# Routing the last rows of a graph layer while the first expert already runs

## The chip, the cores and the metric

The kernel runs on one core of one Trainium2 chip, as one launch. The metric is the device time of an execution in microseconds (us); a time is given as the median of several executions. One execution was recorded by the hardware profiler; times inside it count from the start of its span. Engines: TensorE (PE; its weight loads are PEld), VectorE (DVE), ScalarE (ACT), GpSimd (POOL) and SyncE (SP), which issues transfers (DMA).

## The reference, cut to what matters

3125 nodes with 256 features each go through four stages, each added to its input:

```
x = x + gat(gat(gat(layernorm(x))))        # three attention layers over the edges, relu between
x = x + top2_experts(layernorm(x))         # 16 experts, hidden 512
x = x + relu(h @ W + sum_of_neighbours(h @ M))    with h = layernorm(x)
x = x + top1_expert(layernorm(x))          # 8 experts on a shared hidden layer of 1024
```

The second stage is the one that matters here:

```
logits = einsum('bsd,de->bse', x, gate_w) + gate_b
probs  = softmax(logits);  top_probs, top_idx = top_k(probs, 2), made to sum to 1
hidden = silu(x @ w1[e]) * (x @ w2[e]);    out = sum over the two experts of weight * hidden @ w3[e]
```

Everything is float32. With the inputs given, the 16 experts get between 306 and 473 of the 6250 (node, expert) pairs, expert 0 gets 473.

## The kernel before

**Attention.** The edges are held as a dense matrix of counts. The nodes that receive are cut into 13 groups (`GROUPS`): groups 0 to 11 of 256 nodes, and a small last one of 53. For a group the loop runs over 25 tiles of 128 sending nodes, the steps `s`. In a step VectorE makes `pm` (L1388), 128 senders by 256 receivers, the unnormalised attention, and TensorE multiplies it with the senders' features into `acc` (L1391), one product for each of the group's two tiles of 128 nodes; each product appears as two matmul records. The small group uses `few` instead (L1379, L1381, L1383), six senders' tiles at a time. Six buffers of `pm` let VectorE run ahead.

Work that follows a group is put into a list `later` with a step number, and is issued between the steps of the group after it: `divide` at step 8 (division by the sum of weights, in place of a softmax, and the addition of x, into `y_out`), and in the third layer `norm` at 9, `gate` at 11 and `send` at 14. The engines execute in the order in which this loop issues, each its own queue.

**Router.** `norm` takes mean and variance, and stores the group's x to `sums` in DRAM. `gate` makes the normalised `row`, transposes it, multiplies with the gate's weights (L638). `send` picks the two largest logits of 16, makes weights, counts in `pre` how many rows each expert has so far, gets each row's `rank` among its expert's rows by two matmuls (L661), turns it into a place `g_to` (L670), and writes each row to its places in `rows` in DRAM with indirect transfers of GpSimd (L677), two for each tile of 128 nodes. Every expert has its own stretch of places. ScalarE needs three functions with tables of their own here: Sqrt in `norm`, Exp in `send`, and SiLU in the experts.

**finish** sums the counts up, and works out by some twenty small VectorE operations (to L721) a table of extra places: expert e's first 384 rows (`EACH` = 3 tiles) are done with the expert itself, the others in slots of 64 between and behind the experts. While VectorE does this, 32 matmuls of `keep_warm` occupy TensorE (L558).

**Experts.** `routed_experts` goes through the experts 0 to 15. `turn(e)` loads 384 rows `xs` (L745, on SP) and transposes them (L750, L751). `first` multiplies with w1 and w2 in four pairs (j, u) of 128 hidden features (`ps_h`, L775, 32 records), and makes `hid` by SiLU (L778) and a product (L779). `second` multiplies with w3 (`ps_o`, L790), weights the result to `y` (L793), and adds its rows into `sums` by indirect transfers (L795), one for each tile. The weights of expert e are loaded by `fetch`, three transfers of 512 KB. When all are done, x is loaded back from `sums` for the third stage.

What is allocated from one pool waits for the last reader of the buffer that it takes over, transfers included. Groups of large blocks (`block(big)`, two of them) are shared by the stages in turn.

Of the kernel before, what the change touches and what calls it, by code (L numbers as in the profile page):

```python
# [22 lines left out]
P = 128  # L23
# [543 lines left out]
class Router:  # L567
# [6 lines left out]
    def __init__(self, tc, cp, ident, eps, iota, count, rows, sums, gate_w, gate_b, table):  # L574
        nc = self.nc = tc.nc
        self.table = table
        self.tc, self.ident, self.eps, self.iota, self.rows, self.sums = tc, ident, eps, iota, rows, sums
        self.before, self.every = count
        self.gw = cp.tile([P, KD, NX0], F32, name="gate_w")
        nc.sync.dma_start(self.gw, gate_w.rearrange("(k p) e -> p k e", p=P))  # L580
        self.gb = cp.tile([P, NX0], F32, name="gate_b")
        nc.sync.dma_start(self.gb, spread(gate_b, NX0))
        spare = cp.tile([P, D], F32, name="spare")
        nc.gpsimd.memset(spare, 0.0)
        for q in range(0, CAP0, P):
            nc.sync.dma_start(sums[NP + q:NP + q + P], spare)

        self.real = cp.tile([P, NT], F32, name="real")
        nc.gpsimd.memset(self.real, 1.0)
        nc.gpsimd.affine_select(self.real, self.real, pattern=[[-P, NT]], compare_op=OP.is_gt, fill=0.0, base=N,  # L590
                                channel_multiplier=-1)

        self.off = cp.tile([P, NT], F32, name="off")
        nc.vector.tensor_scalar(self.off, self.real, -float(NX0 * NP), float(NX0 * NP), op0=OP.mult, op1=OP.add)

        self.pre = cp.tile([P, NT + 1, NX0], BF16, name="pre0")
        nc.gpsimd.memset(self.pre[:, 0], 0.0)
        self.first = cp.tile([P, NX0], F32, name="first0")
        nc.gpsimd.iota(self.first, pattern=[[NP, NX0]], base=0, channel_multiplier=0,
                       allow_small_or_imprecise_dtypes=True)  # L600
        self.node = cp.tile([P, NT], F32, name="node0")
        nc.gpsimd.iota(self.node, pattern=[[P, NT]], base=0, channel_multiplier=1,
                       allow_small_or_imprecise_dtypes=True)

    def group(self, wp, rp, pp, x, t0, n):
# [7 lines left out]
        def norm():  # L613
            for i, t in enumerate(tiles):
                st = wp.tile([P, 6], F32, name="g_st")
                nc.vector.bn_stats(st, x[:, t])
                nc.vector.bn_aggr(mv[:, i], st)
            nc.scalar.activation(rstd[:, 1], mv[:, :, 1], AF.Sqrt, bias=self.eps)
            table(nc, wp, rstd[:, 1], AF.Exp)
            nc.vector.reciprocal(rstd[:, 0], rstd[:, 1])  # L620
            nc.sync.dma_start(self.sums[t0 * P:(t0 + n) * P].rearrange("(t p) f -> p t f", p=P), x[:, t0:t0 + n])
# [3 lines left out]
        def gate():  # L625
            pz = pp.tile([P, n, NX0], F32, name="ps_z")
            for i, t in enumerate(tiles):
                row = rp.tile([P, ROW0], F32, name="row")
                nc.vector.tensor_scalar(row[:, :D], x[:, t], mv[:, i, 0:1], rstd[:, 0, i:i + 1], op0=OP.subtract,
# [11 lines left out]
        def send():  # L641
# [7 lines left out]
            if t0 + n == NT - 1:  # L649
# [8 lines left out]
            for i, t in enumerate(tiles):  # L658
                nc.vector.tensor_tensor(self.pre[:, t + 1], self.pre[:, t], sel[:, i], op=OP.add)
            rank = pp.tile([P, n, NX0], F32, name="ps_z")  # L660
            nc.tensor.matmul(rank, self.before, sel, start=True, stop=False)  # L661
            nc.tensor.matmul(rank, self.every, self.pre[:, t0:t0 + n], start=False, stop=True)
# [18 lines left out]
        return norm, gate, send  # L681

    def finish(self, cp, pp, over):
# [5 lines left out]
        nc.scalar.copy(self.pre[0:1, 0], total)  # L689
        keep_warm(nc, pp.tile([P, (NT + 1) * NX0], F32, name="ps_x"), self.every, self.pre.rearrange("p t e -> p (t e)"), 32)  # L690
# [32 lines left out]

def routed_experts(tc, x, room, ident, rows, sums, places, w1, w2, w3, load):
# [10 lines left out]
    with tc.tile_pool(name="rw", bufs=3) as ep, tc.tile_pool(name="rx", bufs=2) as xp, \  # L735
# [5 lines left out]
        def turn(e):  # L741
            xs = xp.tile([P, nq, ROW0], F32, name="xs")
            for q, n in ((0, nq),) if e else ((0, 1), (1, 1), (2, nq - 2)):
# [10 lines left out]
        def fetch(e, behind):  # L754
# [3 lines left out]
            if 0 < e < 3:  # L758
# [3 lines left out]
            dma = (nc.sync if 0 < e < 3 else nc.scalar).dma_start  # L762
# [95 lines left out]
        turned = turn(0)  # L858
        behind = turned[1][:, 0, 0:1]
        for e in range(NX0):  # L860
            a, b, o = fetch(e, behind)
            if e == 2:
# [214 lines left out]
FINISH = [(0, 20), (2, 16), (4, 4), (5, 16)]  # L1077
TERMS = 18
# [96 lines left out]
def dense_attention(tc, dram, counts, x_in, big, ident, eps, layers, src, dst, rows, high, make_router, over, count):  # L1175
# [10 lines left out]
    with tc.tile_pool(name="dw", bufs=1) as cp, tc.tile_pool(name="dwl", bufs=2) as wl, \  # L1186
# [3 lines left out]
        with tc.tile_pool(name="dp", bufs=6) as pmp, tc.tile_pool(name="ds", bufs=2) as sp, \  # L1190
# [81 lines left out]
            def terms(now, a):  # L1272

                c, n = GROUPS[a]
# [36 lines left out]
            for i in range(3):  # L1311
                last = i == 2
                bt_i = bt
                if last:
# [4 lines left out]
                    y_out = block(big)  # L1319
                    nc.gpsimd.memset(y_out[:, NT - 1], 0.0)  # L1320
# [23 lines left out]
                for a, (c, n) in enumerate(GROUPS):  # L1344
                    if apart_now and a < APART:
                        continue
                    tiles = [(q, (c + q) // P, min(P, n - q)) for q in range(0, n, P)]

                    edges = counts_of(counts, a)
                    ahead = list(pairs[a + 1]) if i == 0 and a + 1 < len(GROUPS) else []  # L1350
                    ready = []
                    tau = tau_next or terms(now, a)
# [8 lines left out]
                    for s in range(NT):  # L1361
                        now_step[0] = (a - APART) * NT + s
                        if s == (EARLIER if apart_now else TERMS):
                            if a + 1 < len(GROUPS):
                                tau_next = terms(now, a + 1)
                            else:
                                tau_next = None if last else terms(nxt, 0 if apart_now else APART)
# [17 lines left out]
                        else:  # L1385
# [4 lines left out]
                            for j, (q, t, r) in enumerate(tiles):  # L1390
                                nc.tensor.matmul(acc[:r, j, :D + 1], pm[:, q:q + r], now.h[:, of, :D + 1], start=(s == 0),  # L1391
                                                 stop=(s == NT - 1))
                        while ready and ready[0][0] <= s:
# [22 lines left out]
                    def divide(tiles=tiles, acc=acc, rest=rest, b=bt_i, last=last):  # L1416
# [13 lines left out]
                        for j, (q, t, r) in enumerate(tiles):  # L1430
                            if last:
                                to, add = y_out[:r, t], rest[j][:r]
# [9 lines left out]
                    sooner = 2 if a == len(GROUPS) - 2 else 5 if i == 0 and a == len(GROUPS) - 1 else 0  # L1442
                    later.append((8 - sooner, divide))
                    if last:
                        norm, gate, send = router.group(wp, rp, zp, y_out, tiles[0][1], len(tiles))
                        later += [(9 - sooner, norm), (11 - sooner, gate), (14 - sooner, send)]
# [28 lines left out]
            for _, what in later:  # L1475
                what()
            router.finish(wp, zp, over)
# [8 lines left out]
    return y_out  # L1486
# [525 lines left out]
def routed(ctx: ExitStack, tc: tile.TileContext, i: dict, out: bass.AP, over):  # L2012
# [12 lines left out]
    with tc.tile_pool(name="counts", bufs=1) as kp:  # L2025
        counts = kp.tile([P, NT * ((len(GROUPS) - 1) * PAIR + 64)], U8, name="counts")
        x = dense_attention(tc, dram, counts, i["x"], big, ident, eps, layers, i["src"], i["dst"], (rows0, rows),
                            over[:, 3:4], lambda cp: Router(tc, cp, ident, eps, iota, count, rows0, sums,
                                                            i["L0_ffn_gate_w"], i["L0_ffn_gate_b"], more), over[:, 0:1], count)
        with tc.tile_pool(name="s0", bufs=1) as sp:  # L2030
            ws, wm = (sp.tile([P, KD, D], F32, name="s_" + n) for n in "WM")
            hidden = hidden_weights(nc, early, *(i["L1_ffn_" + n] for n in ("W1", "b1", "Wg", "bg")), x[:, 0, 0:1])
            room = block(big).rearrange("p t d -> p (t d)")
            xnT = room.rearrange("p (k n) -> p k n", k=KD)
            routed_experts(tc, x, room, ident, rows0, sums, more, *(i["L0_ffn_" + n] for n in ("w1", "w2", "w3")),
# [96 lines left out]
```

## Time and profile before

| | |
|---|---|
| median of 6 executions | 1898.14 us (1895.28 to 1901.55) |
| the profiled execution | 1903.16 us |
| its span | 1901.4 us |
| TensorE busy in the span | 1792.8 us, 94% |
| VectorE / ScalarE / GpSimd busy | 1018.2 / 725.8 / 489.7 us |
| mean granted TensorE clock | 0.976 |
| third layer's group 11, last matmul | ends 1073.2 us |
| small group's last matmul | ends 1080.4 us |
| first expert's first matmul | starts 1104.8 us |
| second expert's first matmul | starts 1122.9 us |

How to read the lines that follow. A line of a chain of waits is: start in us, duration, engine, what it writes, line of the program, number of instructions. A line of a table by stretches is: the stretch, its length, busy time and number of instructions of each engine, the clock that TensorE was granted (1.00 is full speed), the share of the DMA engines in use, GB/s. A line of a table of groups is: program line, engine, operation, tile written <- tiles read, shapes, number | busy us, mean ns of one | idle time of the engine just before, and what ended it. The busy time of matmul records overlaps with that of the next: from start to start they are shorter than their mean.

### The profile page before, as it was taken

How to read it: one execution, taken by the hardware profiler on the slowest of the kernel's cores; microseconds unless marked ns; L12 is line 12 of the kernel's file. 1: busy time of each engine (PE TensorE's matmuls, PEld its weight loads, DVE VectorE, ACT ScalarE, POOL GpSimd, SP SyncE). 2: the span in 40 equal slices, each digit the busy share in tenths (PEclk: the TensorE clock that was granted, in tenths of full speed). 3: DMA queues.
4: the chain of work that ended last, by engine and by line, in shares of the span. 5: the costliest groups of instructions: out<-in, count | busy, mean ns of one | idle time of the engine just before them, and what ended most of it. 6: DMA issues, size and time to landing. Idle time of an engine off the chain costs nothing. (4 is left out here: it accounts for less than half of the span.)

```text
span 1901.4 us, 27323 instructions
## 1 busy us (share of the span) xinstructions
PE 1792.8 (94%) x9249; PEld 1400.3 (74%) x9249; DVE 1018.2 (54%) x2865; ACT 725.8 (38%) x2078; POOL 489.7 (26%) x636
## 2 busy tenths in 40 slices
PE   6999999999698888999999799999989999999997
PEld 4788888887576777788888666666668887555886
DVE  6888888875376666677777622222244222324221
ACT  3767666761001011222222211121127999444221
POOL 4210110000665655023333322333310000132122
PEclk9999999999799989999999999999999999999999
DMA  3111214766332323121111175877430000743764
GB/s 114 32 46 49 82 45 172 300 247 237 82 89 76 88 69 81 32 57 45 45 46 45 68 233 151 248 194 193 106 87 1 1 1 1 240 159 125 226 210 126
DMA packets 118370, 211.50 MB, mean 111 GB/s; under 512 B 14843, under 2 KB 80929, under 8 KB 118184
## 3 DMA queue, kind: packets, MB, share of 16 engines
q1 hardware_dynamic: 78228, 130.30, 20.4%
q0 software_dynamic: 24848, 56.84, 11.5%
q10 hardware_dynamic: 15138, 22.44, 3.6%
q8 instruction: 79, 1.29, 0.3%
q14 instruction: 77, 0.63, 0.1%
HBM read 118.61 MB, written 93.00 MB: 111 GB/s over the span
## 5 line engine op out<-in xcount | busy, mean ns | idle before, releaser
L1391 PE MATMUL acc<-big,pm 128*128 128x257 f32 x3400 | 798.0, 386 | 17.0 <-issue 13.3
L1391 PEld LDWEIGHTS acc<-big,pm 128*128 128x128 f32 x3400 | 634.9, 192 | 111.4 <-issue 17.3
L1388 DVE SCALAR_TENSOR_TENSOR pm<-tau,big,counts 128x256 f32<-128x256 f32 x850 | 397.3, 485 | 144.5 <-PE acc L1391 111.6
L1933 POOL DMA_INDIRECT apart_row<-apart_rows,apart_who x172 | 174.8, 1016 | 117.4 <-DVE apart_acc L1959 58.3
L775 PE MATMUL ps_h<-xsT,w 128*128 128x384 f32 x512 | 170.1, 491 | 0.6 <-ACT xsT L751 0.6
L1543 PE MATMUL acc<-msg,cr 128*128 128x512 f32 (+1 forms) x625 | 158.1, 404 | 0.0
L775 PEld LDWEIGHTS ps_h<-xsT,w 128*128 128x128 f32 x512 | 97.5, 191 | 67.8 <-issue 3.4
L1543 PEld LDWEIGHTS acc<-msg,cr 128*128 128x128 f32 (+1 forms) x625 | 114.9, 185 | 29.2 <-ACT cr L1539 1.1
L1539 ACT ACTIVATE cr<-counts 128x256 fp32r<-128x256 uint8 (+1 forms) x325 | 130.5, 402 | 14.3 <-PE acc L1543 7.0
L1799 ACT CAST counts<-acc_c 128x500 uint8<-128x500 f32 (+1 forms) x155 | 95.9, 677 | 94.8 <-PE acc_c L1789 94.6
L1024 PE MATMUL ps_y<-t_wd,hsT 128*128 x480 | 108.8, 380 | 0.0
L1161 PE MATMUL ps_m<-we,yT 128*128 128x258 f32 (+1 forms) x248 | 73.2, 416 | 34.1 <-ACT yT L1291 23.6
L1774 DVE TENSOR_TENSOR ohk<-iota_k,key 128x2016 f16<-128x2016 f16 (+1 forms) x79 | 94.3, 1193 | 20.2 <-PE acc_c L1789 20.0
L778 ACT ACTIVATE silu<-ps_h 128x384 f32<-128x384 f32 x64 | 31.4, 490 | 183.9 <-PE ps_h L775 183.9
L795 POOL DMA_INDIRECT sums<-y,who x48 | 74.7, 1556 | 93.4 <-DVE y L793 80.4
L1291 ACT ACTIVATE yT<-ps_m 128x256 f32<-128x256 f32 (+1 forms) x25 | 9.5, 379 | 230.0 <-remote 103.8
L1024 PEld LDWEIGHTS ps_y<-t_wd,hsT 128*128 128x128 f32 x480 | 88.8, 190 | 11.1 <-issue 0.3
L779 DVE TENSOR_TENSOR hid<-silu,ps_h 128x384 f32<-128x384 f32 x64 | 35.4, 554 | 113.9 <-PE ps_h L775 106.5
L1768 ACT ACTIVATE ohs<-iota_s,low 128x128 f16<-128x128 f16 x286 | 94.0, 400 | 0.0
L930 PE MATMUL ps_H<-big,t_w 128*128 128x512 f32 (+1 forms) x224 | 93.1, 552 | 0.8 <-ACT H L932 0.5
L790 PE MATMUL ps_o<-w,hid 128*128 128x256 f32 x384 | 87.2, 379 | 0.0
L1789 PEld LDWEIGHTS <-ohs 128*128 128x128 f16 x1250 | 77.7, 98 | 10.9
(380 smaller groups left out, 2167.8 us busy)
## 6 DMA issues: line engine op xcount, KB each, us to landing
rows<-empty SPq DMA_DIRECT2D x16, 2564.0 KB
w<-in_L_ffn_w_dram ACTq DMA_DIRECT2D x42, 512.0 KB
hs<-rows SPq DMA_DIRECT2D x29, 641.0 KB
big<-in_L_ffn_w_dram SPq DMA_DIRECT2D x30, 512.0 KB
rows<-empty SPq DMA_DIRECT2D x16, 516.0 KB
t_wd<-in_L_ffn_Wd_dram SPq DMA_DIRECT2D x8, 1024.0 KB
xs<-rows SPq DMA_DIRECT2D x15, 387.0 KB
bias<-in_L_ffn_bd_dram SPq DMA_DIRECT2D x30, 128.0 KB
```

The lines of the kernel that those rows point to most:

```text
L775: nc.tensor.matmul(ps, w[:, k, j * P:(j + 1) * P], xsT[:, k], start=(k == 0), stop=(k == KD - 1))
L790: nc.tensor.matmul(ps, hid[:, j, q * P:(q + 1) * P], o[:, j], start=(j == 0), stop=(j == nh - 1))
L930: nc.tensor.matmul(ps[:, :n], a[:, k, j * P:(j + 1) * P], xnT[:, k, c:c + n], start=(k == 0), stop=(k == KD - 1))
L1024: nc.tensor.matmul(ps, hsT[:, j], d[:, ds(e, 1), j, :].rearrange("p o f -> p (o f)"), start=(j == 0), stop=(j == nh - 1))
L1388: nc.vector.scalar_tensor_tensor(pm[:, :n], tau[:, :n], now.rho[:, of:of + 1], edges[:, of, :n], op0=OP.max, op1=OP.mult)
L1391: nc.tensor.matmul(acc[:r, j, :D + 1], pm[:, q:q + r], now.h[:, of, :D + 1], start=(s == 0), stop=(s == NT - 1))
L1539: nc.scalar.activation(cr[:, :n], edges[:, s, :n], AF.Copy, accum_out=seen[:, a * NT + s:a * NT + s + 1])
L1543: nc.tensor.matmul(acc[:r, j].rearrange("p h d -> p (h d)"), cr[:, q:q + r], msg[:, s].rearrange("p h d -> p (h d)"), start=(s == 0), stop ...
L1768: nc.scalar.activation(far[:, i], self.iota_s, AF.Abs, scale=-1.0, bias=self.low32[:, batch, i:i + 1])
L1774: nc.vector.tensor_tensor(to[:, i:tiles].rearrange("p t (x u) -> p t x u", u=2), iota.rearrange("p (x u) -> p x u", u=2)[:, None].to_broad ...
L1799: nc.scalar.copy(to[:, :, d0 % PAIR:d0 % PAIR + whole * WIN].rearrange("p s (u d) -> p u s d", u=whole), acc[:, :whole])
L1933: nc.gpsimd.indirect_dma_start(out=row[:, j], out_offset=None, in_=self.table[:, :], in_offset=bass.IndirectOffsetOnAxis(ap=self.who[:, q ...
```

## The change

Three things move.

1. **Order of the third layer.** The list of parts is groups 0 to 9, then the small group, then group 10, then group 11 as two parts of 128 nodes (called 11a and 11b here). The small group's norm, gate, choose and send are issued in group 10 rather than in its own follower's first steps. `send` is cut in two, `choose` (up to the counts) and `send` (rank, places, rows). `divide` writes into a tile of its own for each part, where it wrote into one block for all nodes.

2. **Places of expert 0.** After group 10 has been sent, with two parts (256 nodes) still to come, `reserve` raises the first free place of expert 0 to at least 384, so that the rows of the last two parts lie behind the first 384. With these inputs expert 0 has 438 rows by then, so that nothing is raised.

3. **Expert 0 early.** A `FirstExpert` holds the weights (loaded at the start of the third layer) in one of the large blocks. Its 384 rows are loaded once group 10 has been sent. After the last attention matmul its matmuls are issued in a fixed order (`manual_schedule`) between divide, norm, gate, choose and send of 11b. `finish` comes behind, without the 32 matmuls of `keep_warm`; `routed_experts` starts with expert 1, whose weights and rows are now loaded by SP.

Besides, the weights of the fourth stage's hidden layer are loaded in the third layer, at group 2, and the transfers that were held behind a first tile are shifted by one expert.

```diff
+    def reserve(self, pp):
+        ps = pp.tile([P, 1], F32, name="ps_z")
+        nc.tensor.matmul(ps, self.every, self.pre[:, self.sent, 0:1], start=True, stop=True)
+        nc.vector.tensor_scalar(self.bump, ps, -1.0, float(EACH * P), op0=OP.mult, op1=OP.add)
+        nc.vector.tensor_scalar(self.bump, self.bump, 0.0, None, op0=OP.max)
+        nc.vector.tensor_tensor(self.first[:, 0:1], self.first[:, 0:1], self.bump, op=OP.add)
...
@@ Router.finish
-        nc.scalar.copy(self.pre[0:1, 0], total)
-        keep_warm(nc, pp.tile([P, (NT + 1) * NX0], F32, name="ps_x"), self.every, self.pre.rearrange("p t e -> p (t e)"), 32)
+        places = cp.tile([1, NX0], F32, name="more_total")
+        nc.vector.tensor_copy(places, total)
+        nc.vector.tensor_tensor(places[:, 0:1], places[:, 0:1], self.bump[0:1], op=OP.add)
+        total = places
...
+class FirstExpert:
+    def __init__(self, tc, room, wp, ident, rows, sums, w1, w2, w3):
...
+        for to, w in ((self.a, w1), (self.b, w2), (self.o, w3)):
+            nc.sync.dma_start(to, w[0].rearrange("(k p) h -> p k h", p=P))
+    def load(self):
+        self.nc.sync.dma_start(self.xs, self.rows[:EACH * P].rearrange("(q p) f -> p q f", p=P))
+    def turn(self, pp):
+        for q in range(EACH):
+            ps = pp.tile([P, KD, P], F32, name="ps_m")
+            for k in range(KD):
+                nc.tensor.transpose(ps[:, k], self.xs[:, q, k * P:(k + 1) * P], self.ident)
+            nc.scalar.copy(self.xsT[:, :, q * P:(q + 1) * P], ps)
+        nc.gpsimd.tensor_copy(self.who, self.xs[:, :, D])
+    def first(self, ap_, j, u):
+        if u == 0:
+            self.ps = ap_.tile([P, 2, CHUNK], F32, name="acc")
+        for k in range(KD):
+            nc.tensor.matmul(self.ps[:, u, :EACH * P], (self.a, self.b)[u][:, k, j * P:(j + 1) * P], self.xsT[:, k],
+                             start=(k == 0), stop=(k == KD - 1))
+        if u:
+            nc.scalar.activation(self.hid[:, j], self.ps[:, 0, :EACH * P], AF.Silu)
+            nc.vector.tensor_tensor(self.hid[:, j], self.hid[:, j], self.ps[:, 1, :EACH * P], op=OP.mult)
+    def second(self, pp, q):
+        ps = pp.tile([P, D], F32, name="ps_m")
+        for j in range(nh):
+            nc.tensor.matmul(ps, self.hid[:, j, q * P:(q + 1) * P], self.o[:, j], start=(j == 0), stop=(j == nh - 1))
+        y = self.wp.tile([P, D], F32, name=f"yT{q % 2}")
+        nc.vector.tensor_scalar(y, ps, self.xs[:, q, D + 1:D + 2], None, op0=OP.mult)
+        independent(self.tc, "sums0", nc.gpsimd.indirect_dma_start(
+            out=self.sums[:, :], out_offset=bass.IndirectOffsetOnAxis(ap=self.who[:, q:q + 1], axis=0),
+            in_=y, in_offset=None, bounds_check=NP + CAP0 - 1, oob_is_err=True, compute_op=OP.add))
...
@@ routed_experts
-        turned = turn(0)
+        weights = fetch(1, None)
+        turned = turn(1)
...
-        for e in range(NX0):
-            a, b, o = fetch(e, behind)
-            if e == 2:
+        for e in range(1, NX0):
+            a, b, o = weights if e == 1 else fetch(e, behind)
+            if e == 3:
...
+LATE = 2
+LAST_PARTS = PARTS_OF[:10] + PARTS_OF[12:] + PARTS_OF[10:11] + [(11, 11 * PAIR + q, P) for q in (0, P)]
...
@@ dense_attention, third layer
-                        norm, gate, send = router.group(wp, rp, zp, y_out, tiles[0][1], len(tiles))
-                        later += [(9 - sooner, norm), (11 - sooner, gate), (14 - sooner, send)]
+                        more = NT if short else 0
+                        if len(parts) - at == 2:
+                            sooner = 4
+                        later += [(8 - sooner, divide), (9 - sooner + more, norm), (11 - sooner + more, gate),
+                                  (14 - sooner + more, choose), (14 - sooner + more, send)]
+                        if len(parts) - at == LATE + 1:
+                            later += [(14, lambda: router.reserve(zp)), (14, expert.load)]
...
             for _, what in later:
                 what()
+            with tc.manual_schedule():
+                expert.turn(pp)
+                divide()
+                expert.first(ap_, 0, 0)
+                norm()
+                expert.first(ap_, 0, 1)
+                expert.first(ap_, 1, 0)
+                gate()
+                expert.first(ap_, 1, 1)
+                expert.first(ap_, 2, 0)
+                choose()
+                expert.first(ap_, 2, 1)
+                expert.first(ap_, 3, 0)
+                send()
+                expert.first(ap_, 3, 1)
+                for q in range(EACH):
+                    expert.second(pp, q)
             router.finish(wp, zp, over)
```

## The prediction, made before the changed kernel ran

> **What bounds the kernel now.** I read the page's busy table first (TensorE is busy for 94% of a span of 1901.4 us), then the table by stretches of time, to find where the missing 6% lies near the change.
>
> ```profile
> core 0: us, PE busy (x) PEld busy (x) DVE busy (x) ACT busy (x) POOL busy (x), PEclk, DMA share, GB/s
> 1050.00:1073.00 23.00, 23.00 (x115) 19.75 (x113) 16.60 (x62) 4.96 (x10) 5.73 (x12) 1.00 0.09 32
> 1073.00:1105.00 32.00, 20.18 (x116) 10.71 (x115) 19.40 (x101) 8.77 (x21) 10.24 (x22) 0.79 0.32 106
> 1105.00:1390.00 285.00, 285.00 (x1147) 187.10 (x1148) 64.58 (x123) 53.24 (x110) 89.73 (x88) 0.99 0.69 185
> ```
>
> The third attention layer (first row) and the routed experts (third row) are bound by TensorE. Between them it idles, and the clock falls to 0.79. The last attention matmul ends at 1080.41, and the first expert matmul starts at 1104.82. The chain of waits shows what fills these 24.4 us:
>
> ```profile
> 1087.56 0.43 DVE row L629
> ...
> 1094.41 0.23 DVE g_to L670 x2
> ...
> 1099.42 0.19 DVE more L721
> ...
> 1101.13 3.13 DMA xs<-rows
> ...
> 1104.82 12.28 PE ps_h L775 x32
> 1117.10 0.66 PE ps_x L750 x6
> 1117.76 5.18 PE ps_o L790 x24
> 1122.94 10.32 PE ps_h L775 x32
> ```
>
> Routing of the last rows (to g_to), the table of extra places (to L721), the load of expert 0's rows, expert 0, expert 1. Expert 1's first matmul starts 42.5 us after the attention's last (1122.94 - 1080.41), and its 32 end at 1133.26, after 52.85 us. From there on both kernels do the same 15 experts, so I compare this one interval. Expert 0's 12.28 against expert 1's 10.32 is the clock:
>
> ```profile
> 1104.80:1106.00 1.20, 1.18 (x2) 0.63 0.72 209
> 1106.00:1107.00 1.00, 1.00 (x3) 0.50 0.90 303
> ...
> 1109.00:1110.00 1.00, 1.00 (x5) 1.00 1.05 378
> ```
>
> ```profile
> 1408.90:1412.00 3.10, 1.77 (x5) 0.50 1.05 353
> 1412.00:1415.70 3.70, 3.60 (x11) 0.50 1.04 342
> ```
>
> The fourth column is the granted clock. After about 5 us of idle it was half from 1105.1 to 1108.5, which cost 1.96. After 6.2 us of idle later in the kernel TensorE restarted at 1410.15 and ran at half until 1415.7: at most 2.8 lost.
>
> **What the change trades.** It takes expert 0's matmuls and the wait for its rows out of the 42.5 us, but expert 0 now stands between the last attention matmul and expert 1, mixed with the last part's routing; the attention's end moves as well. My frame for the new order starts where group 10's matmuls started before (1026.5), so that the old attention end is 53.9.
>
> Attention. Before: group 10, group 11, small group = 53.9. After: small group, group 10, halves 11a and 11b.
> - Small group: 7.24 from 1073.17, of which some 0.9 is idle before the end. With a group behind it that idle fills: 6.3 (6.0 to 6.6).
> - Group 10: one group's period was 23.8. It now carries the small group's gate and rank too, about 1.0 of TensorE by the x12 and x8 gate rows (four records of one tile 0.4, two transposes 0.2, a rank 0.33), and a stall of about 0.5 where TensorE's rank matmul waits for VectorE's choice: 25.3 (24.3 to 26).
> - The halves. TensorE: 50 steps of two matmuls at 0.217 from start to start, the same 21.7 as one group, and about 3 for two routings: 24.6. VectorE:
>
> ```profile
> L1388 DVE SCALAR_TENSOR_TENSOR pm<-tau,big,counts 128x256 f32<-128x256 f32 x20 | 9.9, 503 | 3.6 <-PE acc L1391 3.6
> ```
>
> one pm a step, 0.396 from start to start at 256 wide, and the halves need 50 of 128 wide instead of 25. No row has that shape: a dependent 128x32 operation takes 0.22 and a 512-wide one 0.70, and the line through 0.70 and 0.396 gives 0.24. I take 0.26, so 13 where one group had 9.9, with two routings of 5 to 7 (16.60 in the first row less 9.9): about 25, level with TensorE. Neither hides behind the other.
> - TensorE executes in order, and the rank matmul of 11a stands before the last two of 11b; each rank waits for about ten VectorE operations. Halves: 26.1 (24.6 to 29).
>
> What matters more than the halves' end is when expert 0's rows are there. Their load waits for group 10's last row scatter. Its g_to lies, by adding VectorE's queue up, 18.0 after the first matmul of 11a (15.5 if a 128-wide pm costs 0.22 and the small operations overlap as they do where they are independent, 0.11 each; 21 if it costs 0.396). Four scatters take 5.6:
>
> ```profile
> L677 POOL DMA_INDIRECT rows<-row,g_to x9 | 8.8, 979 | 5.5 <-issue 1.8 <-DVE more_end L699 1.7 <-DVE row L629 1.6
> ```
>
> (1.0 each, 1.3 apart). Landing took at most 2.15 before (1097.64 to 1099.8), the load 3.13. On SP the load is behind 11a's store of x, issued earlier. Rows there: 18.0 + 5.6 + 2.15 + 3.2 = 29.0 (26 to 32). So TensorE idles 3 us after the attention. In the frame: 6.3 + 25.3 + 29.0 = 60.6, or 6.7 after the old attention end.
>
> Expert 0's pass, from there. Transposes and copies 1.6. Eight (j, u) of TensorE are 8 x 1.29 = 10.3, but ordered around divide, norm, gate, choose and send of 11b, whose dependent VectorE chain alone was 7.1 from row to g_to (1087.56 to 1094.64), with SiLU's and Exp's tables loaded in turn. My walk in program order: row +5.3, second hid +8.8, choice to +13.5, g_to +16.35, last hid +17.0. TensorE then has three times 1.73 of ps_o: last y +21.6. GpSimd's two row scatters and three scatter-adds (1.55 each, 1.85 apart) end at +24.55. Then a wait that expert 1 did not have before: its xs lies in the space of the y tiles, so its load waits for all three scatter-adds to land.
>
> ```profile
> L795 POOL DMA_INDIRECT sums<-y,who x3: 1546/1546/1546, 1394.8 to 1398.5; - x3
> ```
>
> ```profile
> 1394.81 9.16 DMA sums<-y,who
> ```
>
> The last one began at 1398.5, was issued by 1400.06 and landed at 1403.97: 3.9. So +28.45; issue, load (3.13), transposes and copies 5.4: expert 1 starts at +33.9 (31.5 to 36). TensorE idles some 10 us before it.
>
> Costs at nothing. The finish chain (5 us of VectorE from g_to) lies beside ps_o and the landing; at +23 it has 5 us in hand. Expert 0's weights and hidden_weights move into the third layer, where the DMA share is 0.09. Expert 1's 1.5 MB now goes out on SP behind the attention's end: 4.2 at 378 GB/s, under the scatter-adds' landing; the xs load stands behind it on SP. All expert counts leave room, so the reserve moves no rows. The 32 keep-warm matmuls occupied nobody, but see the clock.
>
> The clock. TensorE idles 3 us before expert 0 and works in short pieces: I take the row's 1.96 (0 to 2). Expert 1 starts cold after 10 us of idle: 2.8, the row with the longer idle (1.7 to 3.4: half of the 3.4 and of the 6.8 us, 1408.9 to 1415.7, that the rows show at half).
> "TensorE: Matmul & The Clock Gate" in the Trainium skill (section on the HAM clock gate) gives a free-running window of about 3.4 us: one idle window halves the clock, one busy window restores it. The rows agree (1105.1 to 1108.5 is 3.4), and it speaks against this change, which makes two such idles of one; by it alone expert 1 would lose 1.7 to 3.4, so the sum would be the same to 1.1.
>
> The table loads.
>
> ```profile
> L552 ACT ACT_TABLE_LOAD  x2: 1283/1283/1283, 1076.2 to 1087.1; - x2
> L552 ACT ACTIVATE table<-g_rstd x2: 202/202/203, 1077.5 to 1088.4; 128x1 f32<-128x1 f32 x2
> ```
>
> The next operation starts 1.3 after the load starts, so I charge 1.28 a switch; three are in the pass.
> "ScalarE: Activation LUTs" (What ACT_TABLE_LOAD costs) adds a drain of 1.38 to each switch; by it the pass would be some 3 to 4 longer. These rows show no drain.
>
> Sum: 6.7 + 33.9 + 1.96 + 1.2 (some 30 hand-overs between engines at the 0.04 that the chain calls issue) = 43.8 to expert 1's start, where it was 42.5; then 10.3 + 2.8 = 13.1. 56.9 against 52.85: 4.1 slower. The profiled execution took 1903.16 (span 1901.4), 5.0 over the median; the difference carries to the median of 1898.14: 1902.2.
>
> **The rivals.** What a measurement of this kernel can tell is about 0.2%, or 3.8 us.
> - Faster: VectorE is not the bound in the halves. If 128-wide pm costs 0.22 and independent operations overlap, g_to comes at 15.5. Then small group 6.0, group 10 24.3, rows at 26.5 (-3.8); no idle and so no slow clock in expert 0 (-1.96); the choice takes the 3.3 of the old chain (1090.47 to 1093.8) instead of 4.75 (-1.4); hand-overs are already in it (-1.2). 4.1 - 8.4 = -4.3: 1893.8. For it: VectorE was busy 16.60 of 23.00. Against it: VectorE gets 25 pm's fixed cost more and the routing of two parts in the same time. It decides from g_to of group 10 within 16 us of 11a's first matmul.
> - Level: the waits are as walked, but the clock stays full in expert 0 and costs expert 1 1.96 as before: 4.1 - 1.96 - 0.84 = 1.3, 1899.4; without the hand-overs 1898.2. For it: the window's phase is chance. Against: an idle of 10 us before expert 1.
> - The change does not do what it says, if the early load waits for later scatters: the program's order shows it waiting for group 10's only. I give it almost nothing; the whole pass would then stand behind the routing, over 10 slower.
>
> **How the numbers follow.** Slower by over 0.2% gets 0.47, level 0.29, the faster rival 0.24. All terms at their good ends give -6.9, all at their bad ends +10.8. The slower case's own range is 1901.9 to 1908; the range reaches down over the level case and the faster rival's middle to 1892.5, and up to 1908.5.
>
> **What would show it.** In the profile after: TensorE's idle before expert 0's transposes (3, rival 0); g_to of group 10 18 after 11a's first matmul; last y to expert 1's first matmul 12, most of it one scatter-add's landing and a load; clock 0.5 when expert 1 starts; 56.9 from the old frame's 53.9 to the end of expert 1's first 32 matmuls, that is 110.8 after group 10's place began. It is wrong if the interval between last attention matmul and expert 1 is under 36, or if time moves anywhere before the third layer or behind expert 1.

## The result, and the profile after

The changed kernel is slower. Its median is 1903.38 us (33 executions, 1892.34 to 1917.3) against 1895.47 us of before (75 executions, 1883.1 to 1907.83); the ratio is 1.0041, 95% interval [1.0029, 1.0053]. The profiled execution took 1899.87 us, with a span of 1898.2 us. That its span is shorter than that of before (1901.4) says nothing on the change: the second attention layer, which the change doesn't touch, took 315.7 us in the profile of before and 309.5 in this one (the small group's first matmul less the layer's first). So all that follows is measured in one frame: zero is the first matmul of group 9 plus 23.82 us, the period of a group. There group 10 began in before, and here the small group begins (its first matmul comes 0.3 us earlier).

In this frame expert 1's first 32 matmuls end at 107.4 in before and at 110.9 after. From there to the end of the last expert's `ps_h` matmuls both take 258.55 us, and from there to the end of the span both take 509.6. Inside the frame the profile after shows this, first as a table by stretches (start:end, length, busy time and instructions of PE, PEld, DVE, ACT, POOL, then clock, DMA share, GB/s):

```profile
1025.70:1049.90 24.20, 24.16 (x123) 20.89 (x123) 19.09 (x90) 7.79 (x18) 6.73 (x14) 1.00 0.09 31
1049.90:1075.80 25.90, 25.30 (x125) 20.31 (x123) 23.25 (x119) 9.14 (x18) 8.95 (x17) 1.00 0.15 49
1075.80:1079.10 3.30, 0.02 (x1) 0.00 (x0) 1.42 (x5) 0.00 (x0) 0.00 (x0) 1.00 0.60 162
1079.10:1103.20 24.10, 20.22 (x72) 12.49 (x72) 10.77 (x50) 7.90 (x14) 6.72 (x10) 0.93 0.06 22
1103.20:1117.40 14.20, 1.68 (x7) 1.22 (x7) 2.29 (x11) 0.44 (x2) 3.64 (x4) 0.66 0.73 165
1117.40:1130.00 12.60, 12.51 (x34) 7.28 (x35) 1.67 (x3) 2.38 (x6) 1.20 (x9) 0.84 0.98 333
```

The rows are group 10; the two halves of group 11; the wait for expert 0's rows; expert 0 up to its last y; the wait for expert 1's rows; expert 1's 32 matmuls. In the halves VectorE is busy for 23.25 of 25.90, where it was 16.60 of 23.00. TensorE is idle in two places, 3.3 and 14.2 long (less 1.7 of small matmuls). The chain of waits (start, duration, engine, tile, line) names what ends them:

```profile
1067.73 0.23 DVE g_to L691 x2
...
1073.06 2.65 DMA rows<-row,g_to
...
1075.73 3.35 DMA big<-rows
...
1080.92 4.26 PE acc L782 x8
...
1097.41 0.17 DVE g_to L691
...
1101.23 4.27 DMA sums<-yT,big
...
1105.71 5.44 DMA sums<-yT,big
...
1112.68 4.29 DMA xs<-rows
...
1117.49 12.47 PE ps_h L851 x32
```

Group 10's g_to, the landing of its row scatters and the load end the first wait; the scatter-adds of expert 0 (L795) and the load of expert 1's rows the second. Expert 1's 12.47 against 10.3 is the clock again (fourth column):

```profile
1081.00:1083.60 2.60, 2.60 (x4) 0.50 0.28 102
1083.60:1086.00 2.40, 2.40 (x9) 0.96 0.00 0
1118.00:1121.00 3.00, 3.00 (x6) 0.50 0.83 246
1121.00:1122.00 1.00, 1.00 (x4) 0.84 1.04 399
```

After 3.3 us of idle expert 0's first four matmuls run at half, after the long wait expert 1's until 1121.

### The profile page after: what moved, and what is told of

It is laid out like the page before. It is cut to its first block, busy times and chain, and to the rows that moved or that the text cites. A ratio compares the mean times of both kernels' runs of the same rounds, so it can differ in the third digit from the quotient of the medians.

```text
span 1898.2 us, 27319 instructions
## 1 busy us (share of the span) xinstructions
PE 1787.3 (94%) x9220; PEld 1395.6 (74%) x9220; DVE 1021.9 (54%) x2923; ACT 730.0 (38%) x2084; POOL 491.6 (26%) x636
## 5 line engine op out<-in xcount | busy, mean ns | idle before, releaser
L1471 DVE SCALAR_TENSOR_TENSOR pm<-tau,big,counts 128x256 f32<-128x256 f32 (+1 forms) x875 | 401.2, 477 | 137.7 <-PE acc L1474 110.4
L851 PE MATMUL ps_h<-xsT,w 128*128 128x384 f32 x480 | 159.8, 492 | 0.5 <-ACT xsT L827 0.5
L851 PEld LDWEIGHTS ps_h<-xsT,w 128*128 128x128 f32 x480 | 91.6, 192 | 63.8 <-issue 3.7
L1659 PEld LDWEIGHTS acc<-msg,cr 128*128 128x128 f32 (+1 forms) x625 | 114.7, 185 | 29.2 <-ACT cr L1655 1.2
L1915 ACT CAST counts<-acc_c 128x500 uint8<-128x500 f32 (+1 forms) x155 | 95.9, 677 | 93.8 <-PE acc_c L1905 93.2
L871 POOL DMA_INDIRECT sums<-y,who x45 | 70.0, 1555 | 89.5 <-DVE y L869 81.3
L1905 PE MATMUL acc_c<-ohk,ohs 128*128 128x125 f16 x1250 | 84.5, 218 | 0.0
```

Of the source, the lines that this page charges most:

```text
L851: nc.tensor.matmul(ps, w[:, k, j * P:(j + 1) * P], xsT[:, k], start=(k == 0), stop=(k == KD - 1))
L1471: nc.vector.scalar_tensor_tensor(pm[:, :n], tau[:, :n], now.rho[:, of:of + 1], edges[:, of, :n], op0=OP.max, op1=OP.mult)
L1659: nc.tensor.matmul(acc[:r, j].rearrange("p h d -> p (h d)"), cr[:, q:q + r], msg[:, s].rearrange("p h d -> p (h d)"), start=(s == 0), stop ...
L1905: nc.tensor.matmul(acc[:, u], ohs[:, i], ohk[:, i, :KEYS], start=(t == 0), stop=(t == TW - 1))
L1915: nc.scalar.copy(to[:, :, d0 % PAIR:d0 % PAIR + whole * WIN].rearrange("p s (u d) -> p u s d", u=whole), acc[:, :whole])
```

## The experiments

Eleven runs were made, in three lots, each lot on one chip with its own runs of before; e8 and e9 are the two kernels unchanged. The table gives places in the frame, each from the kernel's own profile, and the ratio to before with its interval. "Pass starts" is expert 0's first transpose (its first matmul where expert 0 is not early); it can lie a little ahead of the end of the attention, because matmul records overlap. The pass is the time from there to expert 1's start.

| | attention ends | pass starts | expert 1 starts | its 32 take | they end | ratio of the times |
|---|---|---|---|---|---|---|
| before | 54.6 | 79.0 | 96.9 | 10.5 | 107.4 | |
| after | 56.8 | 60.1 | 98.4 | 12.5 | 110.9 | 1.0041 [1.0029, 1.0053] |
| e1, order only | 56.6 | 78.1 | 96.6 | 10.5 | 107.1 | 1.0023 [0.9996, 1.0049] |
| e2, y apart | 56.7 | 60.3 | 95.9 | 12.5 | 108.3 | 1.0034 [1.0008, 1.0061] |
| e3, load sooner | 57.0 | 56.8 | 94.4 | 13.0 | 107.4 | 0.9994 [0.9970, 1.0018] |
| e4, whole last group | 54.6 | 57.8 | 100.4 | 12.0 | 112.3 | 1.0044 [1.0016, 1.0072] |
| e5, e2 and e3 | 56.2 | 56.0 | 90.6 | 11.7 | 102.3 | 0.9990 [0.9968, 1.0013] |
| e6, and `most` early | 56.7 | 57.3 | 89.7 | 12.3 | 101.9 | 0.9979 [0.9962, 0.9995] |
| e7, and keep_warm | 56.4 | 57.0 | 89.1 | 10.6 | 99.6 | 0.9964 [0.9943, 0.9985] |
| e8, before again | 54.4 | 78.6 | 94.9 | 10.5 | 105.4 | 0.9993 [0.9970, 1.0017] |
| e9, after again | 56.0 | 59.2 | 97.4 | 11.8 | 109.2 | 1.0024 [1.0003, 1.0046] |
| e10, after with keep_warm | 56.7 | 59.9 | 97.0 | 11.4 | 108.4 | 1.0022 [1.0005, 1.0039] |
| e11, before without it | 54.4 | 79.2 | 96.7 | 10.5 | 107.2 | 1.0021 [1.0003, 1.0039] |

**e1, the new order of the attention alone.** The parts are as in after; expert 0 and its load, the reserve and the first-expert class's weights are out, keep_warm is in, and `routed_experts` starts at expert 0.

```diff
-                            later += [(14, lambda: router.reserve(zp)), (14, expert.load)]
+                            nc.vector.memset(router.bump, 0.0)
...
-            with tc.manual_schedule():
-                expert.turn(pp)
...
+            for what in (divide, norm, gate, choose, send):
+                what()
...
-        for e in range(1, NX0):
+        for e in range(NX0):
```

> The new order of the third layer alone (small group before group 10, group 11 in two parts); expert 0 goes through routed_experts as before, with keep_warm. Theory (the loss lies in the wait for expert 0's rows, in its pass and in expert 1's cold start): the last attention matmul comes 2.5 us later in the frame (57.1 instead of 54.5 after the small group's or group 10's start), the routing behind it handles one tile instead of three and is shorter by 2 to 4; in all within 0.2% of before (-2 to +2 us). Rival (the split of group 11 makes VectorE the bound and is itself the loss): slower than before by 4 us or more.

Measured: the attention ends 2.1 later, and the routing behind it takes 21.5 instead of 24.4 (78.1 less 56.6; 79.0 less 54.6). Expert 0's 32 matmuls took 12.85, expert 1 ends 0.3 before its place in before. The times don't decide between same and slower: the interval reaches from 0.8 us faster to 9.3 slower, and so holds the rival's 4. In the frame the new order costs 2.1 and gives 2.9 back, so it isn't the loss there.

**e2, expert 0's y apart from expert 1's rows.** They stand in the space of expert 0's first weights, which are used up by then.

```diff
-        y = self.wp.tile([P, D], F32, name=f"yT{q % 2}")
+        y = self.y[q]            # room[:, q * D:(q + 1) * D]
```

> As after, but expert 0's y stand in the space of its first weights, so that expert 1's rows no longer wait for the scatter-adds to land, only for the last row scatters and the table of extra places. Theory: the load starts at the end of the table (about 26.5 us after expert 0's rows are there, instead of 32.3), shares the DMA engines with expert 1's weights, and expert 1 starts 4 to 6 us earlier: 0.2 to 0.3% faster than after, 1 to 4 us slower than before. Rival (expert 1's weights or the cold clock end that wait too): under 2 us gained.

Measured: expert 1 starts 2.6 earlier, less than either end of what was expected and more than the rival. SyncE's own waits show that the cause of the wait is gone. First after, then e2 (us in total, times, longest):

```profile
SPq L839 <- PE ps_m L1600: 24.8, 1, 24.8
SPq L821 <- DMA sums<-yT,big: 5.6, 2, 4.7
```

```profile
SPq L840 <- PE ps_m L1601: 25.4, 1, 25.4
```

The load (L821 in after) waited for the scatter-adds; in e2 it doesn't. Its first piece is issued at 1109.95 instead of 1111.35, which in the frame is 4.8 earlier (87.5 against 92.3; 5.8 were expected). Two things stand right ahead of it there: the last operation of the table of extra places, `more` L744, ends at 1109.71, and SyncE itself comes free late. Its queue holds expert 1's weights ahead of the rows, and these wait (the line above) for TensorE's last transpose of `most`, a check of the largest logit (L1601):

```profile
1108.63 0.38 SPq L840 DMA_DIRECT2D w<-in_L_ffn_w_dram  x1
1109.07 0.47 SPq L841 DMA_DIRECT2D w<-in_L_ffn_w_dram  x1
1109.95 2.42 SPq L822 DMA_DIRECT2D xs<-rows  x4
```

So the weights travel just when the rows do, and the rows are slow: from the load's first issue to expert 1's first matmul it takes 8.3 here, 6.1 in after and 5.0 for expert 0 in before. That is where 2.2 of the 4.8 go. In time the gain can't be told from none (its ratio's interval holds that of after).

**e3, expert 0's rows one part sooner.** Reserve and load are issued when the small group has been sent.

```diff
-                        if len(parts) - at == LATE + 1:
+                        if n <= P // 2:
                             later += [(14, lambda: router.reserve(zp)), (14, expert.load)]
```

> As after, but expert 0's 384 places are reserved and its rows loaded one part sooner, after the small group has been sent. Theory: the rows land some 20 us before the attention ends, TensorE's idle of 3.3 us before expert 0 goes, and with it the slow clock of its first matmuls (1.4): 4 to 5 us faster than after. Rival (the pass is set by the last part's routing on VectorE and ScalarE, not by the rows): expert 0 starts earlier, but g_to of 11b stays at the same distance from the last attention matmul less 1 us, and under 2.5 us are gained.

Measured: the idle before expert 0 is gone (its first transpose overlaps the attention's last matmul), the granted clock stays at 1.00 through its first matmuls, and expert 1 ends at 107.4, 3.5 before after. What TensorE waited for, in after and then in e3 (us in total, times, longest):

```profile
PE ps_x L826 <- DMA xs<-rows: 11.2, 1, 11.2
PE ps_m L773 <- DMA big<-rows: 3.3, 1, 3.3
PE ps_z L682 <- DVE g_sel L671: 2.0, 1, 2.0
```

```profile
PE ps_x L826 <- DMA xs<-rows: 10.0, 2, 9.6
PE ps_z L682 <- DVE g_sel L671: 2.0, 1, 2.0
```

The second line of after is missing in e3, the others are much as they were. 4 to 5 were expected; expert 1 starts 4.1 earlier, and its colder start (13.0) took part of that. The kernel is level with before.

**e4, group 11 in one part.**

```diff
-LATE = 2
+LATE = 1
-LAST_PARTS = PARTS_OF[:10] + PARTS_OF[12:] + PARTS_OF[10:11] + [(11, 11 * PAIR + q, P) for q in (0, P)]
+LAST_PARTS = PARTS_OF[:10] + PARTS_OF[12:] + PARTS_OF[10:12]
```

> As after, but group 11 stays one part of 256 nodes (the reserve then keeps its whole 256 rows out). Theory: the attention ends 2.1 us earlier (23.8 for the last group instead of 25.9), group 10 is sent at step 10 of 25, so that the rows are there about when it ends (idle 0 to 1.5 instead of 3.3); in expert 0's pass the routing of two tiles costs 1 to 1.5 more on VectorE and two more row scatters (2.6 on GpSimd) ahead of the scatter-adds: 0 to 4 us faster than after. Rival (the split pays as meant, by shortening the routing in the pass): 2 us or more slower than after.

Measured: the attention ends 2.2 earlier, as expected. But the rows are not there earlier against its end (3.3 of idle again), and the pass takes 42.5 instead of 38.4. Expert 1 ends 1.4 later than in after: the rival's side, a little short of its 2.

**e5, e2 and e3 together.**

> The edits of e2 and e3 together: expert 0's rows loaded one part sooner, and its y apart from the space of expert 1's rows. Measured from the place where group 10's matmuls begin in before (23.8 us after group 9's), expert 1's 32 first matmuls ended at 107.4 in before, 110.9 in after, 108.3 in e2 and 107.4 in e3. Theory (the waits add up): the last row scatter of 11b lands at about 82 and the table of extra places is ready then, so the load starts 7 us earlier than in e3 and loses 2 of them to expert 1's weights on the same DMA engines: 102 to 103, in time 4 to 5 us faster than before and 8 faster than after. Rival (the weights of expert 1, issued behind the last DVE and PE work of the attention block, end the wait whatever the rows do): 105 or later.

Measured: 102.3, 5.1 before the place in before and 8.6 before after. The waits add up. The pass is 34.6, 3.8 shorter than in after, where e2 had 2.9 and e3 0.9; it starts 4.0 earlier (e3: 3.2). The last 0.8 is a less cold expert 1, which neither edit does. The load is issued 6.6 earlier than in e3, and from there to expert 1's first matmul it takes 8.0 instead of 5.0. As in e2 it comes 0.2 behind `more` and right behind the weights' issue, so the rival's place for the weights is right and its price is not. In time 4 to 5 us faster than before were expected; the ratio of 0.9990 and its interval (6.0 us faster to 2.5 slower) can't tell that from none.

**e6, the transposes of `most` ahead of expert 0's pass.** The block is moved up, unchanged.

```diff
+            ps = pp.tile([4, P], F32, name="ps_m")
+            nc.tensor.transpose(ps, top, ident)
+            most = cp.tile([4, 1], F32, name="most")
...
             for _, what in later:
                 what()
             with tc.manual_schedule():
...
             router.finish(wp, zp, over)
-            ps = pp.tile([4, P], F32, name="ps_m")
-            nc.tensor.transpose(ps, top, ident)
...
```

> e5, and the two small transposes and reductions of `most` (a check of the largest logit) stand ahead of expert 0's pass instead of behind it; the space of expert 1's weights is free that much sooner, so that their 1.5 MB travel during the pass. Theory (in after, e2 and e5 the row scatters' landing and the load of expert 1's rows share the DMA engines with these weights: 4.6 instead of 2.2 to 2.7 us, and 4.3 to 4.9 instead of 3.2): another 2 to 3 us, expert 1's matmuls end at about 100. Rival (the scatters and the load are slow for a reason of their own): within 1 us of e5.

Measured: the pass is 32.4 instead of 34.6, and from the load's first issue to expert 1's first matmul it takes 5.4 instead of 8.0:

```profile
1099.01 0.19 DVE more L744
...
1099.38 0.34 SPq L822
...
1100.74 3.50 DMA xs<-rows
...
1104.77 12.28 PE ps_h L852 x32
```

The load is issued right behind `more` L744, and no sooner after expert 0's start than in e5 (27.0 and 26.7): SyncE sent the weights out at 1079.0 and then stood at the load, so the table alone holds it now. The whole gain is that the rows no longer travel beside the weights. Only 0.4 arrive at the end: the attention ended 0.5 later, expert 0 began 0.6 behind it, and expert 1 was colder by 0.6.

**e7, keep_warm again.**

```diff
         total = places
+        keep_warm(nc, pp.tile([P, (NT + 1) * NX0], F32, name="ps_x"), self.every, self.pre.rearrange("p t e -> p (t e)"), 32)
```

> e6, and the 32 matmuls of keep_warm are back behind the sum of the counts, where TensorE waits for expert 1's rows. Theory: expert 1's 32 matmuls take 10.3 instead of 12.5 us; with e6's gains expert 1 ends at about 98, 8 to 9 us before it does in before, 0.4 to 0.5% faster. Rival (the clock's windows run on their own, and the 7.8 us of matmuls end too early or delay expert 1): no gain over e6, or a loss of up to 2 us.

Measured: expert 1's 32 take 10.59, and end at 99.6. It is the fastest version: 1884.36 us against 1889.54 of before on that chip, 0.9964 [0.9943, 0.9985]. (The interval of e6 lies below 1 too, and the two overlap.) The 32 matmuls end 2.4 before expert 1's first, and the clock stays full in between:

```profile
1094.00:1106.00 12.00, 11.30 (x58) 0.99 0.51 95
1106.00:1108.00 2.00, 1.42 (x6) 1.00 0.67 214
1108.00:1118.00 10.00, 10.00 (x34) 1.00 1.01 328
```

**e8, before again**, as a control.

> The kernel before, unchanged, run as an experiment. In the profiles the time from the third layer's start to the end differs by 3.2 us between before and after, but the medians by 7.9; the second layer took 309 to 317 us in the six profiles, with the same instructions at the same addresses. Theory (the second layer varies from execution to execution, and the profile of before caught a long one): the ratio is within its interval of 1.000, and the second layer of this profile is near 308 to 312. Rival (a kernel run as the second of a pair is slower by some 0.2%, whatever it is): ratio 1.001 to 1.003.

Measured: the ratio is 0.9993 [0.9970, 1.0017]; the second layer took 306.4. Being run as an experiment costs nothing. Expert 0's 32 took 10.6 here, with the same instructions that took 12.3 in the first profile:

```profile
1093.93 10.59 PE ps_h L775 x32
```

So the place where expert 1 ends in before is 105.4 or 107.4, by chance.

**e9, e10 and e11, three more for the clock and the whole.** e9 is the changed kernel as it is, e10 has e7's two lines in it, and e11 is before with keep_warm taken out:

```diff
-        keep_warm(nc, pp.tile([P, (NT + 1) * NX0], F32, name="ps_x"), self.every, self.pre.rearrange("p t e -> p (t e)"), 32)
```

> The changed kernel, unchanged, on one chip with the two below and with before. From the frame (group 9's start plus 23.8) to the end of expert 1's matmuls the profiles gave 110.9 in after and 107.4 and 105.4 in two of before, whose expert 0 ran at half clock in one and at full clock in the other. Theory (the loss is that interval, and the second layer's 300 to 317 us are chance): the interval is 110 to 112 again and the ratio to before 1.002 to 1.0035. Rival (the changed kernel's second layer is longer on average): interval as before, ratio 1.004 or more.

> The changed kernel with keep_warm's 32 matmuls back behind the sum of the counts. Theory (cold starts cost 2.15 in expert 1): they end some 3 us before expert 1's rows come, which is about one window of the clock; expert 1's 32 matmuls take 10.3 to 11.5 instead of 12.5, 1 to 2 us faster than after, unless expert 1's weights wait for them: they stand ahead of the transposes of `most`, which free the weights' space, so that the weights come 6 to 7 us later (about 1111 plus 4 in after's times) and take the gain back. Rival: as e9 or slower by up to 2.

> The kernel before without keep_warm. Theory (in before keep_warm ends 5 us ahead of expert 0 and helps by the window's chance only; the table of places and the rows' load end that wait anyway): expert 0's 32 matmuls take 12 to 12.5 each time, 0 to 2 us slower than before. Rival (keep_warm saves a whole window or more): 3 us or more slower.

Measured: e9 gives 109.2 (below the 110 expected) and 1.0024. e10 is 0.8 better in the frame and the same in time: its keep_warm matmuls end 8 us before expert 1 starts, and expert 1 is still cold (11.4). Here the rows' load goes out ahead of the weights, as was feared. With no weights on the way the last scatter-add lands 2.2 after its issue on GpSimd ends, where in after it took 3.9 (its row in the chain is issue and landing together, 3.72 against 5.44):

```profile
1096.59 0.19 DVE more L745
...
1096.85 3.72 DMA sums<-yT,big
```

The load is issued 2.1 sooner in the frame, but the weights are issued only at 1102.75, and expert 1's first matmul at 1107.62 comes when the first of them has landed. In e11 expert 0 takes 11.8, and expert 1 ends at 107.2, between the two profiles with keep_warm; the time is 1.0021 [1.0003, 1.0039], 0.6 to 7.4 us slower, where 0 to 2 were expected. That fits either side.

## Why the prediction was right, point by point

The forecast was slower by 4.1 us, at 1902.2; measured are 7.9 us between the medians and, in the frame, 3.5 between the two first profiles. That 1902.2 lies so near the measured 1903.38 is in part luck: it started from a median of before of 1898.14 over 6 executions, and over 75 that median is 1895.47.

One slip first. The prediction took 1026.5 for the first matmul of group 10 in before; the trace has it at 1025.86. So its 110.8 is 111.4 in the frame used here, and the old attention end of 53.9 is 54.6. Durations and differences to before aren't touched. The steps:

- **The end of the attention.** Forecast 57.7 from the small group's first matmul, measured 57.1 (56.8 in the frame). Against the old end it was to come 3.8 later and comes 2.2 later. Group 10 took 24.3 instead of 25.3 (its stall was not there), the small group 6.9 instead of 6.3, the halves 25.9 against 26.1. The front text says that the small group's routing moves into group 10; group 9's is there as well, put off over the small group, and both fit.
- **128-wide pm.** Taken as 0.26 from start to start. The chain of after has the row `1066.28 0.26 DVE pm L1471` between others of 0.26 and, behind a small operation, 0.33. VectorE and TensorE came out level, as walked (23.25 and 25.30 busy of 25.90).
- **g_to of group 10.** Forecast 18.0 after 11a's first matmul; it ends at 1067.96, 18.1 after 1049.9. The faster rival needed 16, and fell here.
- **The rows.** Forecast 29.0 after 11a's first matmul, measured 29.2 (1079.08). Idle 3 against 3.3.
- **Expert 0's pass.** 33.9, and 1.96 of cold clock and 1.2 of hand-overs beside it, together 37.1; measured 38.4. The last y comes at +24.1, where 24.8 were walked with those two terms, and from there to expert 1's first matmul it is 14.2 instead of 12. The three scatter-adds on GpSimd took 2.04, 1.83 and 1.55 instead of 1.55 each, and the load 4.29 instead of 3.13.

```profile
L795 POOL DMA_INDIRECT sums<-yT,big x3: 1548/1828/2041, 1101.2 to 1105.7; - x3
```

- **The landing.** Forecast 3.9, and the last scatter-add was issued by 1107.26 and landed at 1111.15, 3.9 again. This was luck, for the two are not the same thing. In before the row that the forecast went by (DMA sums<-y,who, to 1403.97) is longer than the landing: the last scatter-add's issue ended at 1400.06, its data had moved by 1402.4, 2.3 later, and the next load also waited until the engines met behind the branch at L877, TensorE with its last `ps_o` at 1403.9. In after the 3.9 are a landing with the weights on the way; e10 shows 2.2 for it without them.
- **Costs at nothing.** Expert 1's weights were put under the landing at no cost. They did come in time, but they are not free: with them under way the last two scatter-adds land 4.8 and 3.9 after their issue, without them (e10) 2.2 each, and in e2 and e5 they slow the load by some 3. When they travel earlier (e6), 2.2 of the pass goes. This step failed in kind. Only two of the three transfers, 1.0 of the 1.5 MB, went late; the third was issued at 793.5. The table of extra places had time in hand, as said (5.6 us in after); once the scatter-adds are out of the way it stands right before the load, in e2 and e5 to e7.
- **Expert 1's cold start.** Forecast 2.8, measured 2.15 in after and 1.5 in e9. The prediction says that in before half clock came after about 5 us of idle. The trace doesn't have that: keep_warm's matmuls run until 1102.0, and between them and expert 0's first matmul at 1104.82 TensorE is busy for 1.09 of 2.80.

```profile
1094.26 7.76 PE L558 MATMUL ps_x<-pre,every 128*128 128x416 bf16 x32 [0.25 <-ACT pre L689]
1102.89 0.63 PE L750 MATMUL ps_x<-ident,xs 128*128 128x128 f32 x4 [0.87 <-DMA xs<-rows]
```

- **The tables.** The Trainium skill ("ScalarE: Activation LUTs", What ACT_TABLE_LOAD costs) adds a drain of 1.38 to each load. In expert 0's pass there is none: the load before Exp begins at 1093.0 and Exp at 1094.3.

```profile
L662 ACT ACT_TABLE_LOAD  x1: 1283/1283/1283, 1093.0 to 1093.0; - x1
L662 ACT ACTIVATE fm_m<-fm_m x1: 203/203/203, 1094.3 to 1094.3; 128x1 f32<-128x1 f32 x1
```

The sum for the end of expert 1's matmuls, 4.1 later than in before, met 3.5 in the first profile (110.9 against 107.4) and 1.8 in the second (109.2). Terms of both signs cancelled: against before the rows came 1.2 sooner, the pass was 1.3 longer and the cold start 0.6 shorter.

The level rival was not far: e8 and e9 show that chance alone moves the difference between 1.8 (109.2 less 107.4) and 5.5 (110.9 less 105.4). What it took to be faster, e3 shows for the rows and e5 to e7 for the rest: first the wait for a transfer, twice, and the weights beside the load. VectorE, which the faster rival turned on, sets the pace only behind these, with the table of extra places.

What stays open: 1.0041 over all executions is 5.5 to 10 us, and the frame explains 2 to 5.5. On one chip, e9's 1.0024 agrees with the frame. The second layer took between 300.0 and 317.4 us in the profiles, without a pattern between the kernels; whether the rest lies there, or is the mix of chips, no run tells. It isn't special to after: e1, level in the frame, has a ratio of 1.0023, and all the changed kernels but e3 are 1 to 5.5 us slower against before than their frame says when 107.4 stands for before. With e8's 105.4 in its place that excess is on average below 1 us, so part of it may be that the first profile of before caught a late expert 0. The two ways of measuring agree on what the edits undo: from after to e5 it is 8.6 in the frame and about 0.5%, or 9.6, in the ratios.

## What to carry to other kernels

Work pulled forward into a gap brings its own transfers with it: here the gap of 24 us of routing was filled, and two waits for DRAM took its place, one for rows just written and one for results whose only fault was to stand where the next rows were to go. A third price was the next expert's weights, which travelled beside those transfers. Walk each moved load back to the instruction that frees its space and the one that makes its data, and ask for both whether they can come a step sooner, and look what stands ahead of it in its queue; e2 and e3 are one or two lines each, and with two more edits they turn 0.4% slower into 0.4% faster. And keep the idle TensorE warm up to the work itself: matmuls that ended 1.9 and 2.4 us ahead of it (e8, e7) did that, matmuls that ended 2.8, 5.3 and 8 us ahead (before, e1, e10) did not. Each is one profiled execution.

## What the runs showed of the hardware that was not expected

- The cost of a cold start varies from execution to execution. Expert 1's 32 matmuls took 12.5 in after and 11.8 in e9, the same kernel; in e2 to e6, after a wait of the same kind, they took 12.5, 13.0, 12.0, 11.7 and 12.3, and 10.6 when warm (e7). With keep_warm before it, expert 0 took 12.3 in before and 10.6 in e8, again the same kernel, where keep_warm ended 2.8 and 1.9 us ahead. The Trainium skill's free-running window ("TensorE: Matmul & The Clock Gate", the HAM clock gate) fits a spread of this kind.
- How long a scatter-add takes to land goes with what else is on the way. Without the weights in flight each of expert 0's landed 2.1 to 2.9 us after its issue on GpSimd ended (all three in e6, e7 and e10, the first two in e3 and e5); with the weights in flight 3.9 to 5.8 (the last two in after, e2, e4 and e9, the last in e3 and e5; in e2 the rows are on the way as well). The last row scatters of 11b landed 1.3 to 1.4 after theirs in after and e2.
- A scatter-add of 128 rows of 256 floats held GpSimd for 2.04, 1.83 and 1.55 us in after, e2 and e9 (1.84 for the second in those two), and for 1.6, 1.6 and 1.55 in before, e3 and e5. Why the first two differ was not tried.
